# A second Strassen step in four of the seven products of an attention layer's scores

## The chip, the cores and the metric

The kernel runs on one core of a Trainium2 chip. The metric is the device time of one execution in microseconds, the median of several runs. "PE" is the matmul engine, "DVE" the vector engine, "ACT" the scalar (activation) engine, "SP" the engine whose queue issues the transfers.

## The reference

The input is x of 8 images with 512 channels and 32x32 = 1024 positions, all in fp32. Two attention layers follow one another. Layer 0 is a group norm with 8-headed attention and a projection. Layer 1, where the change lies, is a norm over the whole image with single-headed attention over all 512 channels:

```python
q = jnp.einsum('oc,bcs->bos', wq, nf) + bq[None, :, None]
k = jnp.einsum('oc,bcs->bos', wk, nf) + bk[None, :, None]
v = jnp.einsum('oc,bcs->bos', wv, nf) + bv[None, :, None]
attn = jnp.einsum('bci,bcj->bij', q, k) * c ** (-0.5)
attn = jax.nn.softmax(attn, axis=-1)
out = jnp.einsum('bcj,bij->bci', v, attn)
out = jnp.einsum('oc,bcs->bos', wo, out) + bo[None, :, None]
return x + out.reshape(b, c, h, w)
```

The scores are a product of 1024 keys by 1024 queries over 512 channels, for each of the 8 images.

## The kernel before, in words

The kernel goes through the images one by one. For each it runs layer 0 (`layer0`, L690) and then layer 1 (`attention1`, L999). Layer 1 has four stages. The query stage makes q, into which the weights of k are folded, so that the scores need only x on the side of the keys (`make_q`, L1016). The value stage makes v with the output projection folded in (`make_v`, L517, called at L1054). Then come the score stage (`scores`, L1068) and the value-times-probability stage (`values`, L1126).

Every large product is done with one Strassen step in Winograd's form, with seven products of half-sized blocks where a plain block product needs eight. A is what moves through PE (for the scores: q, cut by channels and queries), B what is loaded as weights (x, cut by channels and keys). `finish` (L186) makes the sums S1 to S4 of A's quarters and `Combined.make` (L390) the differences T1 to T4 of B's, all on DVE. `strassen` (L410) runs the seven products through two PSUM banks: `line` takes A11·B11, then S2·T2, S3·T3 and A22·T4 on top of one another, and is copied out by ACT between them (`copied`, L419); `single` takes A12·B21, then S1·T1 with the later S4·B22. A step can't write a bank before its reader is done. `together` (L454) alternates the steps of two such groups, so that PE works on one while the banks of the other are read. `banks` (L98) hands out the banks by two tags, "s" and "o", two of each.

In the score stage a group is one tile of 128 keys against 512 queries, for both halves of keys and of queries at once. There are four such tiles (t of L1068), two at a time, in turn. A product is two matmuls of 512 columns (k of L1070). Each of the four results of a tile is finished by `done` (L1076): for three of them DVE adds bank and copy into a tile p in SBUF (L1079), for the fourth nothing is added; then ACT takes the exponential (L1081); and `add_up` (L1061) adds p to a running sum over the keys on DVE, one result late, through the list `late` (L1083, L1084). The sums become the softmax's denominators: two matmuls with ones (L1140), a check value (L1152), a reciprocal on DVE (L1153) and a spread over the partitions by transfers on SP's queue (L1154), all in the first step of the values.

The order of work on PE, DVE and ACT is the order in which the program is written (`manual_schedule`, L1228); `at_steps` (L466) runs the steps of a stage and calls extra work, the hooks, after steps given by number. Each engine takes its own instructions in that order. The values start with A11·B11 on a bank of tag "s", and their own sums of probabilities and of v come from `finish_values` (L1109), the first call of which stands just ahead of them. Hooks of the values also reload x of the next image and normalise it (L1312 to L1316).

Of the kernel before, what the change touches and what calls it, by code (L numbers as in the profile page):

```python
# [65 lines left out]
def two_attention_blocks(  # L66
# [383 lines left out]
    def in_turn(*groups):  # L450
        for g in groups:
            yield from g

    def together(*groups):  # L454

        groups = list(groups)
        spares.clear()
        while groups:
            for g in list(groups):
                if next(g, g) is g:  # L460
                    groups.remove(g)
                else:
                    yield
        spares.clear()

    def at_steps(steps, hooks):  # L466

        n = -1
        for n, _ in enumerate(steps):
            for hook in hooks.get(n, []):  # L470
                hook()
        assert n >= max(hooks, default=-1)
# [44 lines left out]
    def make_v(w, n2, bs, vs, name):  # L517


        def pairs(t):  # L520
            return t.rearrange("p (u o) -> p u o", u=2)

        def done(i, half, bank, u):
            v = vs[2 * half + n2][:, :, i * 2 * P : (i + 1) * 2 * P]
            if u is None:
                nc.scalar.copy(v, pairs(bank))
            else:
                nc.vector.tensor_tensor(v, pairs(bank), pairs(u), ALU.add)  # L528

        return strassen(by_positions(w, n2, bs), done, f"{name}_{n2}")  # L530
# [119 lines left out]
    def held(value, name, to=None):  # L650

        t = onepool.tile([P, HALF], FP, tag="held", name=f"held_{name}") if to is None else to
        n = next(extents)
        nc.scalar.activation(t, value, AF.Identity, accum_out=extent[:, n : n + 1])  # L654

    def one_over(ps, name):
        inv = accpool.tile([P, HALF], FP, tag="inv", name=f"inv_{name}")
        nc.vector.reciprocal(inv, ps)  # L658
        return inv

    def spread(inv, rows, to, name):


        t = tile2(f"inv_{name}")
        for i in range(P // rows):
            for half, j in to(i):
                nc.sync.dma_start(
                    t[j * rows : (j + 1) * rows, half, :], inv[i * rows : (i + 1) * rows, :]
                )
        return t  # L670
# [328 lines left out]
    def attention1(xs, norm, b, at_values):  # L999
# [13 lines left out]
        combine.take(xs)  # L1013
        bs = combine.parts

        def make_q(c):  # L1016
            def done(i, half, bank, u):
                n, to = c + 2 * i, piece(qs, c + 2 * i, half)
                if u is not None:
                    nc.vector.tensor_tensor(u, bank, u, ALU.add)  # L1020
                    bank = u

                def scaled():
                    nc.scalar.activation(
                        to, bank, AF.Identity, bias=norm.c[:, n : n + 1],
                        scale=vec[:, V_NW1 + n : V_NW1 + n + 1],
                    )

                if i == half == 0:
                    later.append(scaled)  # L1030
                else:
                    scaled()

            return strassen(by_channels(w, c, bs), done, f"q_1_{b}_{c}")
# [2 lines left out]
            0: [lambda: combine.make(1)],  # L1037
            1: [lambda: combine.make(2)],
            2: [norm.mean_of_all, lambda: combine.make(3)],
            4: [norm.deviation, lambda: combine.make(4)],  # L1040
            5: [norm.untaken, lambda: later.pop(0)(), lambda: later.pop(0)()],
        })
        bias = norm.bias()
# [7 lines left out]
                q_parts[f"S{i}"] = tile2(f"s{i}_q_{b}")  # L1051
            finish(q_parts, a21)

        at_steps(together(*[make_v(w, n2, bs, vs, f"v_1_{b}") for n2 in range(2)]), {1: [finish_q]})  # L1054


        ps = [[[tile2(f"p_1_{b}_{j}{k}{i}") for i in range(2)] for k in range(2)] for j in range(2)]
        acc = tile2(f"acc_1_{b}")
        seen, late = [[], []], []

        def add_up(i, p):  # L1061
            seen[i].append(p)
            if len(seen[i]) == 2:
                nc.vector.tensor_tensor(acc[:, i, :], *seen[i], ALU.add)
            elif len(seen[i]) > 2:
                nc.vector.tensor_tensor(acc[:, i, :], acc[:, i, :], p, ALU.add)

        def scores(t):  # L1068
            def multiply(bank, a, b, fresh):
                for k in range(2):  # L1070
                    nc.tensor.matmul(  # L1071
                        bank, bs[b][:, k, t * P : (t + 1) * P], q_parts[a][:, k, :],
                        start=fresh and k == 0, stop=k == 1, skip_group_check=True,
                    )

            def done(i, j, bank, u):  # L1076
                p = ps[j][t // 2][i][:, t % 2, :]
                if u is not None:
                    nc.vector.tensor_tensor(p, bank, u, ALU.add)  # L1079
                    bank = p  # L1080
                nc.scalar.activation(p, bank, AF.Exp, scale=norm.factor)  # L1081
                if late:
                    add_up(*late.pop())  # L1083
                late.append((i, p))  # L1084

            return strassen(multiply, done, f"s_1_{b}_{t}")

        at_steps(in_turn(*[together(scores(t), scores(t + 1)) for t in range(0, NT // 2, 2)]), {})
        add_up(*late.pop())

        tps = {f"T{n}": [tile2(f"t{n}_p_1_{b}_{k}") for k in range(2)] for n in range(1, 5)}
        svs = {f"S{n}": tile2(f"s{n}_v_1_{b}") for n in range(1, 5)}
# [33 lines left out]
        def values(c):  # L1126
            def multiply(bank, a, b, fresh, cols=slice(0, HALF)):
                for kt in range(NT // 2):
                    nc.tensor.matmul(  # L1129
                        bank, v_parts[kt // 2][a][:, kt % 2, c * P : (c + 1) * P],  # L1130
                        p_parts[kt // 2][b][:, kt % 2, cols], start=fresh and kt == 0,
                        stop=kt == NT // 2 - 1, skip_group_check=True,
                    )

            def done(i, j, bank, u):
                first = i == j == 0
                if first and c == 0:
                    ps = spares[0]
                    for half in range(2):
                        nc.tensor.matmul(  # L1140
                            ps[half * HD : (half + 1) * HD, :], ones[:, :HD], acc[:, half, :],
                            start=True, stop=True,
                        )
                chunk = c + 2 * i
                x = piece(xs, chunk, j)
                if u is None:
                    u = tile_u(f"o_1_{b}_{chunk}_{j}")
                else:
                    nc.vector.tensor_tensor(u, bank, u, ALU.add)
                    bank = u  # L1150
                if first and c == 0:
                    held(ps, f"sum_1_{b}")  # L1152
                    invs.append(one_over(ps, f"1_{b}"))  # L1153
                    invs.append(spread(invs[0], HD, lambda i: [(i, r) for r in range(2)], f"1_{b}"))  # L1154

                def add():
                    nc.vector.scalar_tensor_tensor(
                        u, bank, norm.rstd, invs[1][:, j, :], ALU.mult, ALU.mult
                    )
                    nc.vector.scalar_tensor_tensor(  # L1160
                        x, u, bias[:, chunk : chunk + 1], x, ALU.add, ALU.add
                    )
                    if last:
                        store(chunk, j)

                if first:
                    later.append(add)
                else:
                    add()

            def end():

                x = piece(xs, c, 1)
                for tag, cols in [("s", slice(0, 2 * P)), ("o", slice(2 * P, HALF))]:
                    bank = banks(tag, f"ps_end_{tag}")[:, 0, : 2 * P]
                    multiply(bank, "S4", "B22", True, cols)
                    o = last_us[2][:, cols]
                    nc.vector.scalar_tensor_tensor(
                        o, bank, norm.rstd, invs[1][:, 1, cols], ALU.mult, ALU.mult
                    )  # L1180
                    nc.vector.tensor_tensor(x[:, cols], o, x[:, cols], ALU.add)
                    store(c, 1, cols)

            if last and c == 1:
                return strassen(multiply, done, f"o_1_{b}_{c}", us=last_us, end=end)
            return strassen(multiply, done, f"o_1_{b}_{c}")

        def before_end():
# [3 lines left out]
            nc.vector.scalar_tensor_tensor(u, u, norm.rstd, invs[1][:, 1, :], ALU.mult, ALU.mult)  # L1192
            nc.vector.scalar_tensor_tensor(x, u, bias[:, 1:2], x, ALU.add, ALU.add)

        finish_values(1)
        hooks = {n * 2 - 3: [lambda n=n: finish_values(n)] for n in range(2, 5)}
        hooks[5].extend([lambda: later.pop(0)()] * 2)
        hooks[6] = []
        for n, more in at_values.items():
            hooks.setdefault(n, []).extend(more)  # L1200
        if last:
# [529 lines left out]
```

## Time and profile before

| | |
|---|---|
| time, median of 3 runs | 2896.32 us (2894.77 to 2896.39) |
| span of the profiled execution | 2893.6 us |
| granted PE clock, mean over the span | 1.000 |
| score stage of one image (L1071, fourth image) | 48.07 us |
| value stage of one image (L494, same image) | 24.17 us |
| DVE: in-place or two-source add from PSUM, 128x512 (L1079) | 0.691 us |
| DVE: add-up in SBUF, 128x512 (L1066) | 0.684 us |
| ACT: copy from PSUM, 128x512 (L421, score stage) | 0.582 us |
| ACT: exponential, 128x512 (L1081, from SBUF) | 0.722 us |

An instruction's time in the profile runs from its start to the end of its write. Two instructions of one engine in a row overlap at their ends, so their spacing is less than their time. One fp32 matmul stands as two PE instructions in the records. A line of the groups reads: line, engine, operation, output<-inputs, shapes, count, then busy time and mean ns of one, then the idle time of the engine just before such instructions and what ended it.

### The profile page before, as it was taken

The page shows a single profiled execution, that of the slowest core. Times are in us where ns is not written, and L with a number is a line of the kernel's source. Part 1 is how long each engine was busy: PE and PEld are TensorE (multiplying, and loading weights), DVE is VectorE, ACT ScalarE, POOL GpSimd, SP SyncE. Part 2 cuts the span into 40 slices and gives each one's busy share as a digit, 9 for nine tenths or more (in the row PEclk, how much of TensorE's full clock was granted, in tenths as well). Part 3 has the DMA queues.
Part 4 walks back from the last instruction along what each step waited for, and adds up shares of the span by engine and source line. Part 5 has one row for each costly group of instructions (what it writes and reads, how often), then busy time and mean ns, then how long its engine had stood idle before and what let it go on. Part 6 is the DMA issues. An engine that isn't in the chain of part 4 may idle for free.

```text
span 2893.6 us, 34626 instructions
## 1 busy us (share of the span) xinstructions
PE 2886.0 (100%) x14096; PEld 1363.6 (47%) x14096; DVE 1756.0 (61%) x2196; ACT 1091.5 (38%) x1520; POOL 21.0 (1%) x28
## 2 busy tenths in 40 slices
PE   9999999999999999999999999999999999999999
PEld 5434554345533455335553354533545335453354
DVE  5686366763667536676366753577545775537836
ACT  3462314623155231552315522165222642226431
POOL 0000000000000000000000000000000000000000
PEclk9999999999999999999999999999999999999999
DMA  8412122121222203212032121322212222112001
GB/s 273 158 41 73 51 95 92 44 70 51 95 93 47 88 29 113 77 45 91 26 120 75 42 88 33 112 77 47 81 60 86 77 62 82 47 59 66 8 1 38
DMA packets 77655, 210.79 MB, mean 73 GB/s; under 512 B 19888, under 2 KB 20656, under 8 KB 71088
## 3 DMA queue, kind: packets, MB, share of 16 engines
q1 hardware_dynamic: 77344, 208.48, 22.7%
q8 instruction: 112, 1.84, 0.3%
q14 instruction: 55, 0.45, 0.1%
q10 hardware_dynamic: 144, 0.02, 0.0%
HBM read 137.43 MB, written 28.57 MB: 57 GB/s over the span
## 4 chain that ended last, share of the span: by engine, by line
PE 98%; DVE 1%; DMA 0%; SPq 0%; issue 0%; ACT 0%; DVEq 0%
PE s L716 15%; PE ps_o L735 15%; PE ps_v L494 13%; PE ps_s L1071 13%; PE ps_o L1129 13%; PE ps_q L479 13%; PE ps_k L479 6%; PE ps_p L479 6%; PE ps_wvo L596 0%; PE ps_wqk L626 0%; PE ps_o L1140 0%; PE ps_sum L844 0%; PE ps_q L844 0%; DMA inv<-inv 0%; SPq L862 0%; DVE t_p L800 0%
## 5 line engine op out<-in xcount | busy, mean ns | idle before, releaser
L645 ACT ACTIVATE p<-s 128x1024 f32<-128x1024 f32 x512 | 523.6, 1024 | 322.5 <-PE s L716 310.1
L647 DVE TENSOR_TENSOR acc<-acc,p 128x1024 f32<-128x1024 f32 x384 | 469.0, 1221 | 104.0 <-ACT p L645 92.2
L716 PE MATMUL s<-q,k 64*64 64x512 f32 x4096 | 531.4, 590 | 0.0
L735 PE MATMUL ps_o<-p,v 64*64 64x512 f32 x4096 | 528.6, 589 | 0.0
L716 PEld LDWEIGHTS s<-q,k 64*64 64x64 f32 x4096 | 153.9, 133 | 289.0 <-issue 266.1
L735 PEld LDWEIGHTS ps_o<-p,v 64*64 64x64 f32 x4096 | 156.6, 133 | 282.9 <-issue 278.1
L1079 DVE TENSOR_TENSOR p<-ps_s,u_s 128x512 f32<-128x512 f32 x96 | 66.4, 691 | 246.9 <-ACT u_s L421 140.8
L528 DVE TENSOR_TENSOR v<-ps_v,u_v 128x512 f32<-128x512 f32 x96 | 66.2, 689 | 195.2 <-PE ps_v L494 126.3
L421 ACT COPY u_v<-ps_v 128x512 f32<-128x512 f32 x96 | 56.2, 585 | 305.9 <-PE ps_v L494 305.9
L1071 PE MATMUL ps_s<-s_q,t 128*128 128x512 f32 x384 | 167.4, 592 | 0.0
L1129 PE MATMUL ps_o<-t_p,s_v 128*128 128x512 f32 x384 | 166.1, 592 | 0.0
L421 ACT COPY u_q<-ps_q 128x512 f32<-128x512 f32 x96 | 55.8, 581 | 250.4 <-PE ps_q L479 250.4
L647 DVE TENSOR_TENSOR acc<-p,p 128x1024 f32<-128x1024 f32 x64 | 77.8, 1216 | 84.3 <-ACT p L645 84.3
L1081 ACT ACTIVATE p<-p,factor 128x512 f32<-128x512 f32 x96 | 69.3, 722 | 133.0 <-DVE p L1079 133.0
L1071 PEld LDWEIGHTS ps_s<-s_q,t 128*128 128x128 f32 x384 | 73.0, 190 | 91.8 <-issue 91.8
L1129 PEld LDWEIGHTS ps_o<-t_p,s_v 128*128 128x128 f32 x384 | 73.0, 190 | 91.8 <-issue 88.3
L479 PE MATMUL ps_q<-t,w_wqk 128*128 128x512 f32 x256 | 116.0, 597 | 0.0
L479 PE MATMUL ps_p<-t_p,w_p 128*128 128x512 f32 x256 | 114.4, 596 | 0.8 <-DVE inv L658 0.5
L1129 PE MATMUL ps_o<-p,v 128*128 128x512 f32 x256 | 113.3, 595 | 0.0
L494 PE MATMUL ps_v<-w_wvo,t 128*128 128x256 f32 x512 | 113.1, 379 | 0.0
L1071 PE MATMUL ps_s<-q,x 128*128 128x512 f32 x256 | 112.5, 592 | 0.0
L856 DVE RECIPROCAL inv<-inv 128x512 f32<-128x512 f32 x28 | 93.7, 3346 | 22.9 <-ACT inv L654 22.9
(261 smaller groups left out, 3604.6 us busy)
## 6 DMA issues: line engine op xcount, KB each, us to landing
x<-in_x SPq DMA_DIRECT2D x92, 512.0 KB, 7.2
w_qk<-stored_qk SPq DMA_DIRECT2D x14, 1792.0 KB, 7.3
inv<-inv SPq DMA_DIRECT2D x248, 64.0 KB, 2.0
w_wqk<-stored_wqk SPq DMA_DIRECT2D x8, 1792.0 KB, 7.5
fold<-acc SPq DMA_DIRECT2D x56, 256.0 KB, 3.0
w_wvo<-stored_wvo SPq DMA_DIRECT2D x8, 1792.0 KB, 7.4
out<-x SPq DMA_DIRECT2D x28, 512.0 KB, 2.8
w_v<-stored_v SPq DMA_DIRECT2D x7, 1792.0 KB, 7.0
```

Source lines behind the costliest of these rows:

```text
L421: nc.scalar.copy(us[n][:, :width], line[:, :width])
L479: nc.tensor.matmul(bank, w[a][:, k, c * P : (c + 1) * P], bs[b][:, k, :], start=fresh and k == 0, stop=k == 1, skip_group_check=True,)
L494: nc.tensor.matmul(bank[:, u * 2 * P : (u + 1) * 2 * P], bs[b][:, k, n * P : (n + 1) * P], w[a][:, k, :], start=fresh and u == k == 0, sto ...
L645: nc.scalar.activation(p, s, AF.Exp, scale=factor)
L647: nc.vector.tensor_tensor(acc, first, p, ALU.add)
L716: nc.tensor.matmul(s[cols, j, :], flat(ks[pair])[rows, k0 : k0 + HD], qs[pair][rows, g, :], start=True, stop=True,)
L735: nc.tensor.matmul(o[cols, half, :], vs[kt][rows, c0 : c0 + HD], p[rows, j, :], start=kt == 0, stop=kt == NT - 1,)
L856: nc.vector.reciprocal(invs[g], invs[g])
L1071: nc.tensor.matmul(bank, bs[b][:, k, t * P : (t + 1) * P], q_parts[a][:, k, :], start=fresh and k == 0, stop=k == 1, skip_group_check=True,)
L1079: nc.vector.tensor_tensor(p, bank, u, ALU.add)
L1081: nc.scalar.activation(p, bank, AF.Exp, scale=norm.factor)
L1129: nc.tensor.matmul(bank, v_parts[kt // 2][a][:, kt % 2, c * P : (c + 1) * P], p_parts[kt // 2][b][:, kt % 2, cols], start=fresh and kt == ...
```

## The change

Three of the seven products of the scores (A11·B11, S2·T2, S3·T3, which share the bank `line`) stay as they are, in `line(t)`. The other four (S1·T1, A12·B21, S4·B22, A22·T4) take a second Strassen step: each is cut into quarters of 256 queries, 256 keys and 128 channels, and is done as seven products of two matmuls with 256 columns (`twice`). This is for fewer matmuls on PE: 56 half-width ones take the place of 32 full ones per image. The sums and differences of quarters are made on DVE by `halve_a` and `halve_b`, four adds of 128x256 each, eight calls an image: three as hooks of the query stage, three of the value stage, two of the score stage.

The results are no longer kept in a second tile u. ACT copies the three `line` results straight into the tiles p, S1·T1 (`p5`) is added to them by DVE (`with_p5`), and the quarter products are added in place, bank plus tile into tile (`add`). Only `p5` is started with ACT's copies; in the other three every quarter product is a DVE add. Exponentials are taken in place, and the add-ups now stand right behind their exponential (`done`, `c22`), with no list `late`. The order is: key tiles 0 and 1 with p5 between their steps, key tiles 2 and 3 with A12·B21 between, then S4·B22 and A22·T4 alternating. The matmuls and the reciprocal of the denominators move from the first step of the values to a hook after their third (`sums`).

```diff
+        def halve(part, order):
+            quarter = {}
+            for i in range(2):
+                for j in range(2):
+                    k, n = order(i, j)
+                    quarter[f"{i + 1}{j + 1}"] = part[:, k, n * 2 * P : (n + 1) * 2 * P]
+            return quarter
...
+            for n, x, y, op in [
+                (1, "A21", "A22", ALU.add), (2, "S1", "A11", ALU.subtract),
+                (3, "A11", "A21", ALU.subtract), (4, "A12", "S2", ALU.subtract),
+            ]:
+                nc.vector.tensor_tensor(q[f"S{n}"], q[x], q[y], op)
...
@@ hooks of the query stage
+            3: [lambda: halve_b("B21")],
+            6: [lambda: halve_b("T1")],
+            7: [lambda: halve_b("B22")],
@@ hooks of the value stage
+            1: [finish_q], 4: [lambda: halve_a("S1")], 6: [lambda: halve_a("A12")],
+            8: [lambda: halve_a("S4")],
@@ score stage
-        def scores(t):
-            def multiply(bank, a, b, fresh):
...
-        at_steps(in_turn(*[together(scores(t), scores(t + 1)) for t in range(0, NT // 2, 2)]), {})
-        add_up(*late.pop())
+        def exp_of(p):
+            nc.scalar.activation(p, p, AF.Exp, scale=norm.factor)
+
+        def line(t):
+            bank = banks("s", f"ps_s_1_{b}_{t}")[:, 0, :]
+            for a, v, to in [
+                ("A11", "B11", ps[0][t // 2][0]), ("S2", "T2", ps[1][t // 2][0]),
+                ("S3", "T3", ps[0][t // 2][1]),
+            ]:
...
+                nc.scalar.copy(to[:, t % 2, :], bank)
+                yield
+
+        def twice(a, v, tags, i, j, fresh, final):
...
+            def multiply(bank, x, y, start):
+                for u in range(2):
+                    nc.tensor.matmul(
+                        bank[:, u * 2 * P : (u + 1) * 2 * P], v[y][:, u * P : (u + 1) * P], a[x],
+                        start=start and u == 0, stop=True, skip_group_check=True,
+                    )
...
+            def add(bank, r, t):
+                bank = bank.rearrange("p (u q) -> p u q", u=2)
+                nc.vector.tensor_tensor(at(r, t), bank, at(r, t), ALU.add)
+
+            def take(bank, r, t):
+                if fresh:
+                    nc.scalar.copy(at(r, t), bank.rearrange("p (u q) -> p u q", u=2))
+                else:
+                    add(bank, r, t)
+
+            def done(r, t):
+                if final:
+                    exp_of(at(r, t))
+                    if (r, t) in ((0, 1), (1, 0)):
+                        for u in range(2):
+                            add_up(i, ps[j][t][i][:, u, :])
+
+            multiply(line, "A11", "B11", True)
+            take(line, 0, 0)
+            yield
+            multiply(single, "A12", "B21", True)
+            add(single, 0, 0)
+            done(0, 0)
+            yield
+            multiply(line, "S2", "T2", False)
+            take(line, 0, 1)
+            yield
+            multiply(single, "S1", "T1", True)
+            take(single, 1, 1)
+            yield
+            multiply(line, "S3", "T3", False)
+            add(line, 1, 1)
+            done(1, 1)
+            yield
+            multiply(single, "S4", "B22", False)
+            add(single, 0, 1)
+            done(0, 1)
+            yield
+            multiply(line, "A22", "T4", False)
+            take(line, 1, 0)
+            done(1, 0)
+            yield
+
+        def with_p5(i, j, k):
+            to, other = ps[j][k][i], ps[1][k][1] if i == 0 else ps[0][k][1]
+            nc.vector.tensor_tensor(to, to, other, ALU.add)
+
+        def c22(k):
+            with_p5(1, 1, k)
+            exp_of(ps[1][k][1])
+            for u in range(2):
+                add_up(1, ps[1][k][1][:, u, :])
+
+        p5 = twice("S1", "T1", "oo", 1, 1, True, False)
+        at_steps(together(line(0), p5, line(1), p5), {})
+        p2 = twice("A12", "B21", "oo", 0, 0, False, True)
+        at_steps(together(line(2), p2, line(3), p2), {
+            0: [lambda: with_p5(0, 1, 0)], 2: [lambda: c22(0)],
+            6: [lambda: halve_a("A22")], 8: [lambda: halve_b("T4")],
+        })
+        with_p5(0, 1, 1)
+        at_steps(together(
+            twice("S4", "B22", "so", 0, 1, False, True), twice("A22", "T4", "so", 1, 0, False, True)
+        ), {2: [lambda: c22(1)]})
@@ values
+        def sums():
+            ps = room(f"sum_1_{b}", 0)
...
+            held(ps, f"sum_1_{b}")
+            invs.append(one_over(ps, f"1_{b}"))
+            invs.append(spread(invs[0], HD, lambda i: [(i, r) for r in range(2)], f"1_{b}"))
...
-        hooks[6] = []
+        hooks[2], hooks[6] = [sums], []
```

## The prediction

> **What bounds the kernel now.** I read four views of the profile of the kernel before, from coarse to fine. First the page: busy time by engine, and the chain of work that ended last.
>
> ```profile
> PE 2886.0 (100%) x14096; PEld 1363.6 (47%) x14096; DVE 1756.0 (61%) x2196; ACT 1091.5 (38%) x1520; POOL 21.0 (1%) x28
> ...
> PE 98%; DVE 1%; DMA 0%; SPq 0%; issue 0%; ACT 0%; DVEq 0%
> ```
>
> TensorE is never idle and carries 98% of the chain. So a removed matmul pays in full as long as PE doesn't get a wait in its place. Second, the chain in order of time around one image's score stage, and the busy time in that stretch:
>
> ```profile
> 1387.41 48.07 PE ps_s L1071 x112
> ```
>
> ```profile
> 1387.40:1435.40 48.00, 48.00 (x114) 21.21 (x113) 15.85 (x24) 17.26 (x27) 0.00 (x0) 1.00 0.10 38
> ```
>
> The stage is 112 PE instructions (56 fp32 matmuls of 512 columns, two passes each) without a gap: 48.07/56 = 0.858 us a matmul. The columns are PE, PEld, DVE, ACT, POOL, clock, DMA: DVE is busy 15.85 of 48.00, so there seems to be room for vector work. Third, the groups by shape, for prices:
>
> ```profile
> L494 PE MATMUL ps_v<-w_wvo,t 128*128 128x256 f32 x512 | 113.1, 379 | 0.0
> L1079 DVE TENSOR_TENSOR p<-ps_s,u_s 128x512 f32<-128x512 f32 x96 | 66.4, 691 | 246.9 <-ACT u_s L421 140.8 <-PE ps_s L1071 106.1
> L1081 ACT ACTIVATE p<-p,factor 128x512 f32<-128x512 f32 x96 | 69.3, 722 | 133.0 <-DVE p L1079 133.0
> L1121 DVE TENSOR_TENSOR t_p<-p,p 128x1024 f32<-128x1024 f32 x32 | 38.9, 1217 | 0.0
> ```
>
> Fourth, DVE's timeline, for the spacing of its instructions and for what a wait on ACT looks like:
>
> ```profile
> 1408.05 0.69 DVE L1079 TENSOR_TENSOR p<-ps_s,u_s 128x512 f32<-128x512 f32 x1 [0.41 <-PE ps_s L1071]
> 1408.66 0.68 DVE L1066 TENSOR_TENSOR acc<-acc,p 128x512 f32<-128x512 f32 x1
> 1409.53 0.69 DVE L1066 TENSOR_TENSOR acc<-acc,p 128x512 f32<-128x512 f32 x1 [0.19 <-ACT p L1081]
> ...
> 1438.21 1.22 DVE L1121 TENSOR_TENSOR t_p<-p,p 128x1024 f32<-128x1024 f32 x1
> 1439.34 0.68 DVE L1117 TENSOR_TENSOR s_v<-v,v 128x512 f32<-128x512 f32 x1
> ```
>
> An independent 128x512 add takes a slot of 0.61 us (1408.05 to 1408.66), a 128x1024 one 1.13 (1438.21 to 1439.34). An add that needs the result just before it takes 0.71 (L800, 1317.67 to 1318.38). DVE and ACT hand over in 0.03 (L1079 starts 1405.47 and lasts 0.69; its exp starts 1406.19). In the kernel before, add_up comes one product late (`late`), so DVE seldom stands waiting for the exp.
>
> **What the skill says.** The Trainium skill, TensorE: Matmul & The Clock Gate, section Architectural detail, says that ACT and DVE are strict FIFO: a DVE instruction that waits holds everything behind it. The trace agrees: in the lines above nothing passes the add at 1409.53. The same page, section What's actually happening, says that after an idle window of about 3.4 us, free-running, the PE clock falls to half until a busy window has passed. PE never idles in the trace of before (clock 1.00), so no row here shows it. VectorE: DVE Perf Modes, section The TRN2 errata, prices an fp32 tensor_tensor at (N+151)/0.96 ns: 691 for 512, as L1079 has it, and 424 for 256, where L187 to L190 at 128x256 show 416 to 425.
>
> **The change part by part, for one image.** Removed on PE: four products of eight 512-column matmuls become 4 x 7 x 2 matmuls of 256 columns. L494 gives 113.1/512 = 0.221 us a pass and 24.17/112 = 0.216 back to back, so a quarter product (2 matmuls, 4 passes) costs 0.863. PE now needs 12 line steps x 1.716 + 28 quarter steps x 0.863 = 20.6 + 24.2 = 44.8 us instead of 48.07: minus 3.3, or minus 26.5 over 8 images.
>
> Added on DVE: 24 in-place adds instead of 12 (+12 x 0.61), four with_p5 (x 1.13), eight halve calls (four 128x256 adds each; L187 to L190 take 1.47 for such a four, 35.98 to 37.45). Add-ups stay 14. About +7.3 + 4.5 + 11.8 = 24 us. ACT gets 16 copies for 12 and the same exps: free, it was busy 17 of 48.
>
> Six halve calls cost nothing: three fall in DVE's idle gaps of the query stage (1.70 before L297, 1.35 and 1.43 before L1020), three in those of the value stage (3.88, 0.98, 2.76 before L528). The adds behind them start at most 0.5 us later, and PE wants their banks over 1.5 us after that.
>
> Now the order. The changed program's instructions stand in three groups; I follow each queue with 0 = PE's start of the stage. A product is readable 0.20 after PE's last pass (L1081, 1409.77), and PE restarts 0.25 after a DVE read ends (L973 ends 1676.88, matmul at 1677.12).
>
> Group 1 (lines 0 and 1 with p5) ends at 16.3 without a wait; so does group 2 (lines 2 and 3 with p2), at 32.7, since line steps of 1.7 us give DVE time. But p2's last two steps, with their add-ups, already fall behind. Group 3 holds S4·B22 (x) and A22·T4 (y) alternating, with no lines between: PE offers a product every 0.86 us, and every one is a DVE add. DVE from p2's sixth step, each exp followed at once by its own add-ups, so add, exp, two add-ups = 0.69+0.03+0.72+0.03+0.71+0.61 = 2.79:
> - p2.6 with one add-up: 32.0 + 2.08 = 34.1; p2.7: +2.79 = 36.9; with_p5: +1.13 = 38.0.
> - x1, y1, x2: +1.83 = 39.8. c22: 1.22 + exp of 128x1024 + two add-ups. No such exp is in the trace; between 1.02 (L645, from PSUM) and 1.44 (two of L1081) I take 1.07, since L654 has 1.06 for 128x1024 from SBUF: 3.67, to 43.5.
> - y2, x3, y3, x4, y4: +3.05 = 46.5. x5, y5, x6 then wait for PE a little: x6 starts 48.1.
> - x6 +2.79 = 50.9; y6 +2.79 = 53.7; x7's add ends 54.35.
>
> PE meanwhile waits 0.6 (x2, for p2.7's bank), 2.2 (x3, for x1's add), 2.9 (y4, for y2's add behind c22), and 4.1: the values' first product needs x's line bank, free when x7's add has read it. It starts at 44.8 + 9.8 = 54.6. Before it was 48.07: plus 6.5 an image, 8 x 6.5 = plus 52 us. Behind the waiting DVE stand finish_values(1), done at 62.8 and wanted by PE at 68.3: no further wait.
>
> Moving the sums to step 2 puts the reciprocal (3.36) and the reload of x, queued behind the spread on SyncE, 9.5 us later: loads issue 24.9 after the values' start (15.4 before), land 7.2 later at 32.1, where DVE reaches them; the line bank is wanted by about 35. Nothing, or at most 1 us for each of 7 images.
>
> Clock: the 4.1 us wait holds a whole 3.4 us window in (4.1-3.4)/3.4 = 0.2 of cases, and a half-speed window costs 1.7 to 3.4: estimate 8 x 0.2 x 2.5 = 4 us. Sum: 2896.3 + 52 + 4 = 2952.
>
> Bounds: DVE slots at the bare streaming 0.53 and 1.07 us (512 and 1024 over 0.96) give 5.6 an image, 2941; slots at full durations 0.69 and 1.22 give 7.5, 2956.
>
> **The rivals.** (a) DVE hides everything: about 31 us of DVE slots (24 adds, 14 add-ups, four with_p5, two halve calls) against 44.8 of PE, which keeps its gain of 26.5: 2870, faster. For it: 15.85 of 48 busy, and the groups 1 and 2. Against: the load is not even; group 3 has 12.1 us of PE and 16.5 of DVE adds, plus 3.5 standing for four exps, and DVE comes to it 4 us late (38.0 for a product readable at 33.7). (b) The waits inside group 3 stay but the one ahead of the values goes: 5.7 - 3.3 = 2.4 an image, 2915. It needs x7's add to come 4 us earlier, against FIFO order. (c) The clock falls in nearly every image: 8 x 3.4 = 27 on top of 52: 2975. The waits in group 3 lie close together, and no trace tells how much idling is enough.
>
> **How the numbers follow.** Main case 0.70, c 0.15, b 0.08, a 0.05, a chance cancelling 0.02. Range: down past the streaming bound to 2936, up to c at 2976; a and b are left out. Faster 0.05, same 0.02, slower 0.93.
>
> **What would show it.** PE's instructions rise to 14480 and its busy time falls by about 27, yet the span grows. DVE's share of the chain rises from 1% to about 6% (22 us an image), with PE waiting on the in-place add. DVE shows about 0.87 us of idle on ACT before add-ups. The score stage takes about 54.6. A score stage under 48, or PE without waits at the values' first matmul, would prove the walk wrong; a clock under 0.97 would speak for c.

## The result and the profile after

| | before | after |
|---|---|---|
| time, median | 2895.84 us (2894.77 to 2896.39) | 2971.21 us (2969.27 to 2971.91) |
| ratio, 95% interval | | 1.026 (1.0242 to 1.0277) |
| score stage, fourth image | 48.07 us | 54.42 us |
| values, first 40 PE instructions of the products | 17.17 us | 20.09 us |
| granted PE clock, mean over the span | 1.000 | 0.986 |

The stage and the values are measured on the chain, which counts from the end of the matmul before. The 17.17 leaves out the 1.01 us of the denominators' matmuls, which stand among these 40 in the kernel before.

The changed kernel is 75.4 us slower. The prediction was 2952, in a range of 2936 to 2976, so the direction held and the size fell short by 19 us.

First the page of the changed kernel: busy time by engine, and the chain that ended last.

```profile
PE 2901.0 (98%) x14480; PEld 1452.6 (49%) x14480; DVE 1944.7 (65%) x2580; ACT 1110.3 (37%) x1536; POOL 21.0 (1%) x28
...
PE 94%; DVE 4%; ACT 1%; issue 0%; POOL 0%; DVEq 0%; POOLq 0%
```

PE has the 14480 instructions that were foretold and is no longer always busy: 5% of the chain now lies on DVE and ACT. But PE's busy time has *grown* by 15.0 us, although it does less work. That is the first sign that its instructions got longer. Next, PE's waits in the changed kernel (who waited for whom: us in total, times, longest):

```profile
PE ps_o L1245 <- DVE p L1143: 31.2, 8, 3.9
PE ps_l L1133 <- DVE p L1143: 20.0, 8, 2.5
PE ps_s L1133 <- DVE p L1143: 9.8, 8, 2.7
```

Three waits an image, all for the in-place add (L1143), all in the last group of the score stage or at its end. They come to 61.0 us. With the 15.0 that is 76.0, for the 75.6 us by which the profiled span grew (2969.2 for 2893.6).

The chain of the changed kernel in order of time shows how the last group ends in the fourth image (start, us, what):

```profile
1464.56 0.70 DVE p L1143
...
1465.29 0.73 ACT p L1106
...
1466.04 0.70 DVE acc L1103
...
1466.77 0.69 DVE acc L1103
1467.46 0.61 DVE p L1143
...
1470.27 0.61 DVE p L1143
1470.88 0.14 issue
1471.02 20.09 PE ps_o L1245 x40
```

This is the walk's unit of 2.79 us: add, exponential, two add-ups, next add (1464.56 to 1467.38 by DVE's timeline below, 2.82 us). PE stands until 1471.02. The last line, of the same view over a longer stretch, carries the second surprise: the same 40 instructions of the values took 17.17 before (the run of the side parts, below, shows that line). DVE's timeline of the changed kernel shows DVE standing for the exponential:

```profile
1464.56 0.69 DVE L1143 TENSOR_TENSOR p<-ps_s,p 128x512 f32<-128x512 f32 x1 [0.17 <-PE ps_s L1133]
1466.04 1.42 DVE L1103 TENSOR_TENSOR acc<-acc,p 128x512 f32<-128x512 f32 x2 [0.79 <-ACT p L1106]
1467.38 0.68 DVE L1143 TENSOR_TENSOR p<-ps_s,p 128x512 f32<-128x512 f32 x1
1468.85 1.42 DVE L1103 TENSOR_TENSOR acc<-acc,p 128x512 f32<-128x512 f32 x2 [0.79 <-ACT p L1106]
1470.18 0.68 DVE L1143 TENSOR_TENSOR p<-ps_l,p 128x512 f32<-128x512 f32 x1
```

DVE works twice 0.7 us on the add-ups and stands 0.79 before them. The next in-place add, which PE wants, could have run in that time, but stands behind the add-ups in DVE's order.

The groups of the changed kernel give the same durations as before for the vector work, and one row, the first, that doesn't fit; the last line is that row in the kernel before:

```profile
L1245 PE MATMUL ps_o<-p,v 128*128 128x512 f32 x256 | 133.1, 686 | 31.2 <-DVE p L1143 31.2
L1143 DVE TENSOR_TENSOR p<-ps_l,p 128x512 f32<-128x512 f32 x104 | 69.8, 686 | 70.6 <-PE ps_l L1133 70.6
L1103 DVE TENSOR_TENSOR acc<-acc,p 128x512 f32<-128x512 f32 x96 | 66.5, 692 | 42.9 <-ACT p L1106 41.3
...
L1129 PE MATMUL ps_o<-p,v 128*128 128x512 f32 x256 | 113.3, 595 | 0.0
```

The first matmuls of the values are 686 ns long on average, against 595 before. The windows view tells why. Its columns are the stretch, its length, the busy time of PE, PEld, DVE, ACT, POOL, then the granted clock. I set the stretches on the boundaries that the trace's record of the granted clock has; all of them are 3.41 us or a multiple apart.

```profile
1452.54:1455.95 3.41, 0.92 (x4) 0.66 (x4) 3.38 (x6) 0.00 (x0) 0.00 (x0) 1.00 0.00 0
1455.95:1459.37 3.42, 3.42 (x9) 2.72 (x9) 2.21 (x3) 1.87 (x2) 0.00 (x0) 0.50 0.00 0
...
1466.20:1469.61 3.41, 0.91 (x5) 0.46 (x3) 2.55 (x5) 0.72 (x1) 0.00 (x0) 1.00 0.00 0
1469.61:1473.02 3.41, 2.00 (x3) 1.00 (x4) 2.59 (x5) 0.72 (x1) 0.00 (x0) 0.50 0.00 0
1473.02:1476.44 3.42, 3.42 (x6) 1.34 (x5) 2.60 (x6) 0.72 (x1) 0.00 (x0) 0.50 0.00 0
1476.44:1479.85 3.41, 3.41 (x10) 1.50 (x9) 2.92 (x4) 0.59 (x1) 0.00 (x0) 1.00 0.00 0
```

After each window in which PE was busy for only some 0.9 us, the next one runs at half clock. The second such stretch lasts two windows and lies over the values' start. By the clock record this is so in all eight images: 3.41 and 6.83 us at half clock, 82 us in all. By its timeline PE is busy in 70 of these 82 us, and half of that, 35 us, is what the half clock adds to its busy time. That is most of the 41.3 us by which PE's busy time is too long: it grew by 15.0 where it should have fallen by 8 x (48.07 - 44.78) = 26.3 (the 44.78 is measured below). The other 6 us are not accounted for here.

### The profile page after: what moved, and what is told of

Same layout as the page of the kernel before. It is cut to its first block, busy times and chain, and to the rows that moved or that the text cites. A ratio compares the mean times of both kernels' runs of the same rounds, so it can differ in the third digit from the quotient of the medians.

```text
span 2969.2 us, 35729 instructions
## 1 busy us (share of the span) xinstructions
PE 2901.0 (98%) x14480; PEld 1452.6 (49%) x14480; DVE 1944.7 (65%) x2580; ACT 1110.3 (37%) x1536; POOL 21.0 (1%) x28
## 3 DMA queue, kind: packets, MB, share of 16 engines
q1 hardware_dynamic: 77344, 208.48, 22.1%
## 4 chain that ended last, share of the span: by engine, by line
PE 94%; DVE 4%; ACT 1%; issue 0%; POOL 0%; DVEq 0%; POOLq 0%
PE s L716 15%; PE ps_o L735 15%; PE ps_o L1245 14%; PE ps_q L479 13%; PE ps_v L494 13%; PE ps_k L479 7%; PE ps_p L479 6%; PE ps_s L1117 6%; PE ps_l L1133 2%; PE ps_s L1133 2%; DVE acc L1103 2%; DVE p L1143 1%; ACT p L1106 1%; DVE p L1187 1%; PE ps_wvo L596 0%; PE ps_wqk L626 0%
## 5 line engine op out<-in xcount | busy, mean ns | idle before, releaser
L1245 PE MATMUL ps_o<-p,v 128*128 128x512 f32 x256 | 133.1, 686 | 31.2 <-DVE p L1143 31.2
L1106 ACT ACTIVATE p<-p,factor 128x512 f32<-128x512 f32 (+1 forms) x112 | 87.2, 783 | 164.5 <-DVE p L1143 160.5
L1117 PE MATMUL ps_s<-s_q,t 128*128 128x512 f32 x256 | 120.3, 592 | 0.0
L1143 DVE TENSOR_TENSOR p<-ps_l,p 128x512 f32<-128x512 f32 x104 | 69.8, 686 | 70.6 <-PE ps_l L1133 70.6
L1245 PEld LDWEIGHTS ps_o<-p,v 128*128 128x128 f32 x256 | 56.0, 223 | 104.9 <-issue 104.9
L1143 DVE TENSOR_TENSOR p<-ps_s,p 128x512 f32<-128x512 f32 x88 | 59.9, 687 | 71.1 <-PE ps_s L1133 71.1
```

The lines of the kernel that those rows point to most:

```text
L1106: nc.scalar.activation(p, p, AF.Exp, scale=norm.factor)
L1117: nc.tensor.matmul(bank, bs[v][:, k, t * P : (t + 1) * P], q_parts[a][:, k, :], start=a == "A11" and k == 0, stop=k == 1, skip_group_check ...
L1143: nc.vector.tensor_tensor(at(r, t), bank, at(r, t), ALU.add)
L1245: nc.tensor.matmul(bank, v_parts[kt // 2][a][:, kt % 2, c * P : (c + 1) * P], p_parts[kt // 2][b][:, kt % 2, cols], start=fresh and kt == ...
```

## Experiments

All times are medians; the kernel before, run beside them, had 2895.71, 2896.1 and 2896.24 us in the three batches. Differences to the changed kernel are taken to its 2971.21. The questions: is it DVE's order in the last group that holds PE, and only there? And what makes the clock fall, and what does that cost?

### The side parts alone

```diff
  (kernel before, with halve_a/halve_b and their eight calls, and sums() in the values' third step)
+            6: [lambda: halve_b("T1")],
...
+        hooks[2], hooks[6] = [sums], []
```

The halved operands are made and read by nobody; the scores are those of before.

> The kernel before, with the side parts of the change alone: the eight halve calls at the same places (their results aren't used) and the sums of the denominators in the hook of the values' third step. Theory: they lie beside PE's work and cost nothing; 2896 us within 0.2%, the reload of x later by some 9 us without a wait of PE. Rival (the added DVE work of 11.8 us an image, or the reload that lands late, is a part of the loss): up to 2% more.

Measured: 2895.76 us, ratio 1.0001 (0.9992 to 1.0009). The chain of this run in the fourth image, over the score stage and the values' start:

```profile
1387.47 48.07 PE ps_s L1107 x112
1435.54 17.17 PE ps_o L1167 x40
```

The score stage is 48.07 us and the values take as long as before. So eight `halve` calls and the later denominators cost nothing in the kernel before, where DVE and SP's queue have room. The 75 us must come from the new products, their adds and their order; that the side parts stay harmless among these is shown by the next run, which has them too and keeps 24.7 of the foretold 26.5 us of PE's gain.

### The add-ups out of the last group

```diff
-                            add_up(i, ps[j][t][i][:, u, :])
+                            owed.append((i, ps[j][t][i][:, u, :]))
...
-                add_up(1, ps[1][k][1][:, u, :])
+                owed.append((1, ps[1][k][1][:, u, :]))
...
+            4: [lambda: pay(2)], 6: [lambda: halve_a("A22")], 8: [lambda: halve_b("T4")],
...
         finish_values(1)
+        pay(4)
...
+        hooks[0], hooks[2], hooks[6] = [lambda: pay(len(owed))], [sums], []
```

> The changed kernel with all add-ups taken out of the score stage: they are owed, and paid on DVE after the first call of finish_values (four) and after the first step of the values (nine); one pair of tiles 0 and 1 is paid in the middle of the second group. Theory (DVE's in-order queue in the last group sets the end, by its add-ups and by standing for each exp): with the add-ups gone, DVE has 14 adds and two with_p5 against 12.1 us of PE; walking the queues the values start 45.1 after the stage's start instead of 54.6, PE keeps about 3.0 us an image, clock 1.00; 2896 - 24 = 2872 us. Rival (the cost is DVE's total of work, wherever it stands): unchanged, 2971. Rival (the quarter products are slow on PE by themselves, by loads of weights or clock): above 2896.

Measured: 2870.98 us (2870.73 to 2872.04), ratio 0.9916 (0.9902 to 0.993), clock 1.000. It is faster than both kernels, by 24.7 us than the one before. Thirteen of the 14 add-ups of an image now run during the values. The windows view of this kernel, over its score stage in the same image:

```profile
1378.10:1422.88 44.78, 44.77 (x160) 30.07 (x160) 24.02 (x37) 18.76 (x29) 0.00 (x0) 1.00 0.11 41
```

PE is busy for 44.77 of 44.78 us, which is the 44.8 of PE work that the prediction worked out. The same 24 in-place adds are there, at 0.69 us each as before. DVE's group of the add-ups in this kernel shows that DVE no longer stands for the exponentials:

```profile
L1103 DVE TENSOR_TENSOR acc<-acc,p 128x512 f32<-128x512 f32 x96 | 63.4, 688 | 1.9
```

1.9 us of idle time instead of 42.9. So it was the add-ups' place in DVE's order, with the exponential ahead of them, that made the adds too slow; the adds alone keep up with PE.

### The add-ups one result late

The add-ups stay in the stage, but each pair comes one result later, as in the kernel before.

```diff
+        late = []
+
+        def later_up(i, p):
+            for n, t in late:
+                for u in range(2):
+                    add_up(n, t[:, u, :])
+            late[:] = [] if p is None else [(i, p)]
...
-                        for u in range(2):
-                            add_up(i, ps[j][t][i][:, u, :])
+                        later_up(i, ps[j][t][i])
...
-            for u in range(2):
-                add_up(1, ps[1][k][1][:, u, :])
+            later_up(1, ps[1][k][1])
...
+        later_up(0, None)
```

> The changed kernel with each pair of add-ups put one exponential later on DVE, as the kernel before has it; as many instructions, only their order differs. Theory: DVE no longer stands 0.87 us for each exp and 1.2 for the large one; walking the queues, PE's gaps in the last group shrink to about 1.5 and 2.4 us and the values start at 49.3: 1.2 us an image more than before, 2906 us if the clock stays at 1.00, up to 2929 if such gaps are enough to let it fall. Rival (the standing for the exp is harmless, the number of adds is what counts): 2971, values at 54.6.

Measured: 2913.88 us (2912.36 to 2914.88), ratio 1.0064 (1.0049 to 1.008), clock 0.997. The stage takes 48.83 us. PE's timeline of this kernel, at its two waits:

```profile
1432.21 1.13 PE L1141 MATMUL ps_s<-A_twice,T_twice 128*128 128x256 f32 x4 [1.40 <-DVE p L1151]
...
1440.65 15.67 PE L1252 MATMUL ps_o<-p,v 128*128 128x512 f32 x32 [2.13 <-DVE p L1151]
```

The stage is 5.6 us shorter than in the changed kernel. DVE no longer stands for the exponentials: that was four times 0.79 and once 1.22 us (ahead of the add-ups of the 128x1024 one), 4.4 in all. The other 1.2 us are not standing: one add-up fewer comes ahead of the last add that PE waits for (eight for nine, from the point where DVE begins to fall behind), and an add with work right behind it costs its slot of 0.61 us instead of its full 0.69. What is left against the 44.78 fits the add-ups that still stand ahead of that add, though no run takes it apart. So DVE's standing for ACT was 4.4 of the 9.6 us that the changed kernel loses in this stage. By the clock record the clock still fell in five images of eight, 1.7 us each by PE's timeline: 8.5 of the 18.2 us over the kernel before.

### More work for DVE, in the last group and in the first

```diff
+        def more(n):
+            t = tile2(f"more_1_{b}")
+            for u in range(n):
+                nc.vector.tensor_tensor(
+                    t[:, u % 2, :], q_parts["A22"][:, 0, :], q_parts["A22"][:, 1, :], ALU.add
+                )
...
-        ), {2: [lambda: c22(1)]})
+        ), {2: [lambda: c22(1)], 11: [lambda: more(4)]})
```

> Four extra independent 128x512 adds on DVE (0.61 us each, 2.44 in all) in the last group of the score stage, just ahead of the add that the values' first matmul waits for; their result is read by nobody. Theory (DVE's queue in the last group sets the start of the values): the stage grows from 54.58 to 57.0, plus 8 x 2.44 = 19.5: 2991, up to 2 us an image more (3004) if the longer wait costs another stretch of half clock. Rival (the wait is for PE's own or ACT's work, DVE has slack): 2971.

Measured: 2989.35 us (2986.95 to 2989.7), 18.1 more than the changed kernel. Its chain in order of time, ahead of the values:

```profile
1477.00 2.41 DVE more L1187 x4
1479.41 0.61 DVE p L1143
...
1480.16 18.90 PE ps_o L1252 x40
```

The adds stand in the chain with their full 2.41 us, 19.3 over eight images. The longer wait also shifts where the half clock falls: added up image by image, as in the table further down and with what is lost ahead of the values, it costs 21.4 us here and 23.0 in the changed kernel, so that 17.7 of the measured 18.1 are found. The other run makes the same four adds in the first group:

```diff
-        at_steps(together(line(0), p5, line(1), p5), {})
+        at_steps(together(line(0), p5, line(1), p5), {4: [lambda: more(4)]})
```

> The same four extra 128x512 adds on DVE as in the run with them in the last group (2.44 us an image), but in the first group of the score stage, where PE works in line steps and DVE is not full. Theory (only DVE's queue in the last group counts): 2971, no change. Rival (DVE's load over the whole stage counts): plus 19.5, 2991. The prediction's walk has DVE a little behind already at the end of the second group, so a part of it, up to 2 us an image if the lag reaches there, would say that the backlog begins earlier than the walk has it.

Measured: 2971.76 us (2970.47 to 2972.27), like the changed kernel. The same vector work costs 18 us in one group and nothing in the other. DVE's share of the stage (29.77 us of 54.42 in the changed kernel) says nothing; its queue in the last group says everything.

### PE kept busy in its waits

To part the clock from the waits, PE gets useless work in them: two quarter products of the last group are done three times more, and four products go into a bank that has been read already, ahead of the values. DVE's work is unchanged.

```diff
-            multiply(single, "A12", "B21", True)
+            for _ in range(1 + 3 * (name == "A22")):
+                multiply(single, "A12", "B21", True)
             add(single, 0, 0)
...
-            multiply(single, "S1", "T1", True)
+            for _ in range(1 + 3 * (name == "S4")):
+                multiply(single, "S1", "T1", True)
             take(single, 1, 1)
...
-        ), {2: [lambda: c22(1)]})
+        ), {2: [lambda: c22(1)], 13: [again_x] * 4})
```

> The changed kernel, with matmuls that PE repeats in its three gaps of the last group: y's second product three times more, x's fourth three times more, and four quarter products into a bank that is already read, right behind y's last. Nothing that is used later is changed, and no wait is added. Theory (the gaps cost their own 6.5 us an image, and besides let the PE clock fall to half, which slows the first values by 2.9): the gaps are filled, the clock stays at 1.00, the values start 54.6 after the stage as before and run at full speed; 2971 - 8 x 2.9 = 2948 us. Rival (the clock isn't what slows the first values, they are slow for want of data or banks): clock lower or not, 2971 us. Rival (the idle has nothing to do with the clock, more matmuls lower it further): above 2971.

Measured: 2949.35 us (2948.99 to 2951.06), ratio 1.0187 (1.0172 to 1.0203), clock 1.000. The windows view of this kernel, over the score stage and the values' first 40 instructions in the same image:

```profile
1408.13:1462.54 54.41, 53.85 (x201) 37.51 (x200) 29.75 (x46) 18.71 (x29) 0.00 (x0) 1.00 0.09 34
1462.54:1479.95 17.41, 17.41 (x42) 7.56 (x44) 10.77 (x15) 2.50 (x4) 0.00 (x0) 1.00 0.00 0
```

The stage takes 54.41 us as in the changed kernel (54.42), and the values' start 17.41 instead of 20.09. More matmuls make the kernel 21.9 us faster: that is the price of the half clock alone. The other 53.5 us are DVE's backlog, less what PE saves.

### Only the last wait filled, only the earlier ones filled

In one run only the four products ahead of the values stay, in the other only the repeats.

> Four more quarter products (4 x 0.863 = 3.45 us) only in the last wait of the score stage, the 3.90 us ahead of the values; their result is read by nobody. The waits of 2.50 and 1.02 us further up stay. DVE's queue is unchanged, so the values start as before at 54.4 to 54.6 us. Theory: the half clock after the 2.50 us wait costs nothing, since DVE is the bound there, and only the last wait costs the values their 2.9 us: 2971 - 8 x 2.7 = about 2949, with the clock at about 0.99. Rival: the earlier waits bring the fall that the values see: 2971, clock 0.986.

Measured: 2957.38 us (2956.85 to 2958.08), clock 0.995: the values start at full clock in every image, but the kernel is 8 us over the 2949 that I expected. PE's timeline of this kernel, the waits of the last group in the first image and in the second:

```profile
359.09 1.13 PE L1135 MATMUL ps_l<-S_twice,B_twice 128*128 128x256 f32 x4 [2.50 <-DVE p L1145]
...
364.65 1.77 PE L1135 MATMUL ps_s<-A_twice,T_twice 128*128 128x256 f32 x4 [2.71 <-DVE p L1145]
366.22 1.91 PE L1135 MATMUL ps_l<-S_twice,B_twice 128*128 128x256 f32 x4
...
723.27 1.99 PE L1135 MATMUL ps_l<-S_twice,B_twice 128*128 128x256 f32 x4 [2.50 <-DVE p L1145]
...
728.84 1.13 PE L1135 MATMUL ps_s<-A_twice,T_twice 128*128 128x256 f32 x4 [1.02 <-DVE p L1145]
```

In the second image the half clock (1.99 us for a product that takes 1.13 in the first image) comes right after the first wait, over products that PE would have had to wait behind anyway: the next wait shrinks from 2.71 to 1.02, and nothing is lost. In the first image it comes one wait later, over products that DVE is waiting for, and the values start 1.7 us later. That was so in four images of eight, by 1.5 to 1.7 us, 6.6 in all. The last 1.4 of the 8 us are not accounted for. So my reading that the earlier half clock is free held only for the images where it comes early.

> Three more repeats each of one product of A22*T4 (its second) and one of S4*B22 (its fourth), so that PE is busy in the earlier waits of the last group, and only the wait of about 3.9 us ahead of the values stays. Results are the same. Theory A: one wait of this length is enough for the clock to fall in every image: 2971, one half-clock stretch an image. Theory B: what lets the clock fall is the sum of the waits in the last group (2.50 + 1.02 + 3.90), not one of them: 2948, clock 1.00. As the prediction had it (a whole window inside the wait in some images only): between, about 2952 to 2960.

Measured: 2968.54 us (2967.53 to 2968.83), clock 0.991. One wait of 3.90 us alone is enough, in all eight images. This fits theory A: the sum of the waits doesn't matter.

### The phase of the clock's windows

```diff
-            multiply(single, "A12", "B21", True)
+            for _ in range(1 + fresh):
+                multiply(single, "A12", "B21", True)
             add(single, 0, 0)
```

> One more quarter product (0.863 us) an image on PE in the first group of the score stage, where PE is the bound (the second product of S1*T1 done twice), results the same; all that follows is put off by 0.86 us, with the same waits. Theory that waits of this length always cost the 2.9 us: 2971.2 + 8 x 0.863 = 2978, each image with the same two half-clock stretches. Theory that their place against free-running windows of 3.41 us decides: the period of an image goes from 365.23 us (107.0 windows, so that all images meet the same phase) to 366.1 (107.27), the images now differ, and the time lies below 2978: 2956 if the clock never falls ahead of the values, about 2965 to 2970 if in half of the images.

Measured: 2970.54 us (2968.44 to 2974.57): 6.9 us more work on PE, and no more time. The windows view of this kernel, at the values' start in the fourth image (three stretches) and in the fifth (two):

```profile
1464.95:1468.37 3.42, 1.52 (x8) 0.99 (x6) 2.15 (x4) 1.14 (x2) 0.00 (x0) 1.00 0.00 0
1468.37:1471.78 3.41, 1.41 (x4) 0.72 (x5) 2.55 (x5) 0.72 (x1) 0.00 (x0) 1.00 0.00 0
1471.78:1475.19 3.41, 3.41 (x10) 1.50 (x9) 2.59 (x5) 1.31 (x2) 0.00 (x0) 1.00 0.00 0
1830.18:1833.59 3.41, 1.36 (x7) 0.85 (x5) 2.30 (x4) 0.98 (x2) 0.00 (x0) 1.00 0.00 0
1833.59:1837.01 3.42, 1.57 (x2) 0.84 (x3) 2.56 (x5) 0.72 (x1) 0.00 (x0) 0.50 0.00 0
```

The wait is 3.90 us in both. In the fourth image a boundary cuts it nearly in the middle, PE is busy 1.52 and 1.41 us of the two windows, and the clock stays. In the fifth one window has 1.36, and the next runs at half clock (as does the one after it, by the clock record). In the changed kernel an image takes 365.2 us, 107.0 windows, so seven images meet nearly the same phase; here it is 363.5 to 367.4, and the images differ.

From this I formed a rule, that a window with PE standing for about 2.1 us or more of its 3.41 is followed by half clock, and tried it on a wait of another length: the earlier waits filled, and two of the four products in the last one.

```diff
-        ), {2: [lambda: c22(1)]})
+        ), {2: [lambda: c22(1)], 13: [again_x] * 2})
```

> The earlier waits of the last group filled as before (three repeats each of one product of A22*T4 and one of S4*B22), and two of the four products in the last wait, so that of its 3.9 us some 2.2 are left, ahead of the values. Theory (the clock falls after a fixed window of 3.41 us in which PE stood for some 2.1 us or more, as the windows of the runs so far suggest): a wait of 2.2 us gives such a window only where nearly all of it lies inside one, (3.41 - 2.2 + 0.2)/3.41 = 0.4 of the images, each at 1.7 us: 2949.4 + 8 x 0.4 x 1.7 = 2955, and image by image the fall is where one window holds the wait whole. As the prediction had it (a whole window must lie inside the wait): never, 2949, clock 1.00. Rival, any wait of some 2 us is enough: 2949.4 + 8 x 1.7 = 2963.

Measured: 2957.92 us (2956.91 to 2960.74), clock 0.997. The wait ahead of the values is 2.17 us in all images. The windows view of this kernel, the wait in the second image and in the fourth:

```profile
736.50:739.91 3.41, 1.32 (x3) 0.68 (x4) 2.59 (x4) 0.72 (x1) 0.00 (x0) 1.00 0.00 0
739.91:743.33 3.42, 3.42 (x5) 1.33 (x4) 2.56 (x5) 0.72 (x1) 0.00 (x0) 0.51 0.00 0
...
1463.63:1467.05 3.42, 1.73 (x4) 0.87 (x5) 2.56 (x5) 0.72 (x1) 0.00 (x0) 1.00 0.00 0
1467.05:1470.46 3.41, 3.41 (x9) 1.52 (x8) 2.59 (x5) 1.31 (x2) 0.00 (x0) 1.00 0.00 0
```

The clock fell in the five images in which one window held 2.05 us or more of the wait, and in none of the three where it was cut (at most 1.74 us in one window). I had expected 0.4 of the images; which ones was a matter of phase. 2949.4 + 5 x 1.7 = 2957.9.

What the half clock took from the values in each image is read from PE's timeline: from the values' first matmul to that of the next stage, less the 49.35 us without a fall (46.14 in the last image).

| image | 1 | 2 | 3 | 4 | 5 | 6 | 7 | 8 | sum |
|---|---|---|---|---|---|---|---|---|---|
| changed kernel | 2.56 | 2.64 | 2.67 | 2.67 | 2.65 | 2.70 | 2.70 | 2.71 | 21.3 |
| only the earlier waits filled | 1.69 | 2.48 | 2.58 | 2.63 | 2.62 | 2.68 | 2.68 | 2.71 | 20.1 |
| one product more in the first group | 2.63 | 1.69 | 1.69 | 0.14 | 2.48 | 1.70 | 1.69 | 1.69 | 13.7 |
| last wait cut to 2.17 us | 1.70 | 1.69 | 0.00 | 0.00 | 1.70 | 0.00 | 1.69 | 1.70 | 8.5 |

The third row, with its 6.9 us of work and 1.5 lost ahead of the values in the fifth image, is 22.1; the first, with 1.7 in the first image, is 23.0. That is why the two kernels take the same time.

## Why the prediction was right in kind and short in size

**PE's gain.** Right: 44.8 us of PE work was worked out, and the run with deferred add-ups shows 44.78 without a wait.

**DVE's queue in the last group.** Right, nearly to the instruction. With 0 at PE's start of the stage, as the walk has it (1416.44 by PE's timeline, 0.16 ahead of the chain's count): x6's add at 48.1 (walk 48.1), y6's at 50.9 (50.9), x7's at 53.7 (53.7), the values at 54.6 (54.6). The exponential of 128x1024 took 1.15 us, where 1.07 was taken. On the chain the stage gives 8 x 6.35 = 50.8 us and the values' start, 17.41 at full clock against 17.17, another 1.9: together 52.7 for the foretold 52. (The run with filled waits leaves 53.5; the last 0.8 us are not assigned.) The cause is what the prediction named, the strict order of the vector queue (the Trainium skill, TensorE: Matmul & The Clock Gate, section Architectural detail): the late add-ups, the deferred add-ups and the extra adds each moved the stage as that order says.

**PE's single waits.** Foretold 0.6, 2.2, 2.9 and 4.1 us; measured none, 2.50, 1.02 and 3.90. The 1.02 is the 2.9 shortened by the half clock: where that comes later, as in the first image, it is 2.71. The walk of PE was thus less exact than that of DVE; the values' start hangs on DVE's last add, so this didn't matter there.

**The side parts.** Right: the run with them alone costs nothing, and the reload of x, issued later, makes ACT wait 9.0 us in all (13 times) but PE nowhere.

**The clock: the step that failed.** The term "8 x 0.2 x 2.5 = 4 us" measured about 22 to 23: 21.9 as the difference between the changed kernel and the one with filled waits, 23.0 added up image by image. In the product the 2.5 us was nearly right (2.7). The 0.2 was wrong: it was eight of eight. It came from the assumption that a whole window of 3.4 us must lie inside the wait. The runs show that a window in which PE stands for 2.05 us is enough. A wait of 3.90 us then escapes only if it is cut so that neither side holds 2.05, in (2 x 2.05 - 3.90)/3.41 = 6% of phases, as in the fourth image of the run with one product more. The term also left out the half clock behind the earlier wait, which costs 1.7 us in one image of eight here. Putting 23 for 4 into the sum gives 2896.3 + 52 + 23 = 2971.

**The rivals.** Rival c's mechanism, the clock falling in nearly every image, came true beside the main case; the prediction gave it 0.15. Its mark, a clock under 0.97, was set wrongly: 82 us at half clock in 2969 is a mean of 0.986. The time lies nearer to this rival's 2975 than to the main case's 2952, and above the 2956 of the dearer slots. So the range held because it had been drawn up to the rival, not because the clock's term was right. Rival a's time, 2870, is what the deferred add-ups reach, but with thirteen of the add-ups moved into the values. Over the stage as a whole DVE's 29.77 us were never too much, and four more adds in the first group cost nothing; what it lacked was time in the last group. Rival b didn't come.

**The marks.** "PE's busy time falls by about 27" failed, for the clock again: it rose by 15.0. With the same 14480 instructions at full clock, in the run with deferred add-ups, it is 2861.7, a fall of 24.3. DVE's standing before the add-ups is 0.79 us, for 0.87 foretold, and its share of the chain 4%, for about 6.

## What to carry to other kernels

When a matmul engine is given less work, walk the queue of the engine that empties its banks, group by group, since an average of 55% busy hid a group where it was the bound. Work that nobody in the stage waits for (here the running sums, with an exponential ahead of them) belongs behind the stage: moving it turned 2.6% slower into 0.8% faster. And price a wait of PE twice, once for itself and once for the half clock after it; waits well under a whole clock window cost that too (2.13 and 2.17 us of 3.41 here).

## What the runs showed of the hardware that I had not expected

In all the runs here, from 100 us on up to the kernel's end, each window of 3.41 us at full clock in which PE stood for 2.05 us or more, by PE's timeline, was followed by one at half clock (89 such windows), and none in which it stood for 2.00 or less was; in the windows view the bound lies between 1.36 and 1.41 us busy, some 40%. The Trainium skill, TensorE: Matmul & The Clock Gate, section What's actually happening, speaks of an idle window, and its section HAM oscillation has the rule that PE's idle gaps should not be over about 3.4 us. The length of the window agrees, and so does its running free of the kernel; the rule doesn't, as waits of 2.13 and 2.17 us were enough.

A window at half clock with PE standing for 1.3 us or more was followed by another at half clock (33 such windows); with 0.62 us or less the clock came back. That is how a wait that reaches across a boundary, as the 3.90 us ahead of the values does, costs 2.7 us and not 1.7.

The time of a kernel with such waits depends on the phase. One more product an image in the first group, 6.9 us of PE work, left the time as it was (2970.54 for 2971.21), since fewer images lost the whole 2.7 us.
